# Routing count and experts' bias product given a place in TensorE's order behind the shared expert's first units

## The chip, the cores and the metric

The kernel runs on one core of a Trainium2 chip. The time is device microseconds of one execution. Before the change three runs gave 1411.67, 1405.72 and 1407.75 us, median 1407.75. One further execution was recorded by the profiler; it took 1411.43 us, of which the span from the first to the last instruction is 1409.7 us. Engines are called PE (TensorE), DVE (VectorE), ACT (ScalarE), POOL (GpSimd) and SP (SyncE, which issues most DMAs).

## The reference

Two layers on x of 16 x 256 x 256 (float32): cross-attention, a quantised feed-forward, a correlation attention, and at the end a mixture of experts, where the change lies. Cut to that part:

```python
def _moe_forward(x, Wfc_s, bfc_s, Wproj_s, bproj_s, Wr, Wfc, bfc, Wproj, bproj):
    xf = x.reshape(Bb * Tt, C)                     # 4096 tokens, C = 256, hidden 1024
    shared = new_gelu(xf @ Wfc_s + bfc_s) @ Wproj_s + bproj_s
    logits = xf @ Wr                               # 8 experts
    probs = softmax(logits)
    topk_p, topk_i = top_k(probs, 2)
    topk_p = topk_p / sum(topk_p)
    gate = scatter_add(zeros((N, 8)), topk_i, topk_p)
    routed = 0
    for e in range(8):
        routed += (new_gelu(xf @ Wfc[e] + bfc[e]) @ Wproj[e] + bproj[e]) * gate[:, e:e+1]
    return shared + routed
```

The input of this part is the layer norm of x, and its result is added to x.

## The kernel before

The last part works as follows. A third layer norm of x is transposed into `xnT` (hidden size on the partitions, 4096 tokens along the row), block by block of 512 tokens (`norm3`, transposes at L1351, copies at L1352). `gates(h)` makes the router's logits for half of the tokens each (L1363), turns them back (L1375) and finds the two best experts of every token on DVE (L1384, L1385).

Routing sorts the 8192 pairs of token and expert by expert into tiles of 256 or 128 rows. DVE makes one-hot rows of the choices (`hot`, L1405), adds them, and runs prefix sums over the 32 token tiles (`scan`, L1414 and L1415). What is left is a sum over the 128 partitions, and PE does it: two matmuls `pcount` (L1420 with a triangular matrix, L1421 with ones), copied out as `cnt` (L1423). From `cnt` some 35 small DVE steps compute the start of each expert (`at`), the expert of each tile (`ej`, `ei`), and the slot of each pair (`slot_i`, L1461). `ei` is read by SP into registers, one pair of instructions for each of 46 tiles (L1598), `slot_i` is the index list of the indirect DMAs by which POOL scatters the normalised rows into the DRAM buffer `xs_d` (`scatter`, L1500).

Each tile also needs its expert's hidden bias as a column. `oneT` (L1518) is a one-hot of the tile's expert; eight matmuls `pbias` (L1521) multiply it with the bias table; `bsel` (L1525) is the copy of the product in SBUF. The activations of the routed tiles (L1545, `hTr`) read it.

The shared expert runs in 16 units of 256 tokens. `shared_fc(u)` is the hidden part: 16 matmuls `pfs` (two for each of eight hidden chunks, L1537) and a Gelu on ACT for each chunk (L1545, `hTs`). `shared_proj(u)` is the projection: 16 matmuls `pps` (L1579) and an add onto x on DVE (L1593). A separate DVE add puts the bias row onto x (L1688). Twelve units run ahead of the routed experts, and the hidden part of unit u stands ahead of the projection of unit u-1. The scatters come in eight batches of eight DMAs, and batch k is released by the first activation of unit 3+k (`UB = 3`). Then the routed tiles follow (`routed_fc`, `routed_proj`: weights of the tile's expert by SP, L1600 and L1605, the gathered rows by SP, L1613, transposes L1627, matmuls `pfr` L1537 and `ppr` L1639, a scatter to `ys_d` by POOL, L1665), and at the end the last four shared units beside `combine`, which gathers the two results of every token (L1718) and adds them weighted onto x on DVE (L1726).

The order of the instructions on each engine is chosen by a scheduler, which goes by the program's text as priority and by its estimate of when operands are ready; each engine then works through its list in that order, and an instruction that waits for a semaphore holds the ones behind it. In one earlier stretch PE's order is written out by hand; around this change it isn't. `tc.issue_after(ins)` keeps what is inside it behind `ins` in the list of their engine. In the list of PE before the change the two `pcount` matmuls stand behind two matmuls of unit 0's projection (and a third, which stands earlier, between transposes), with thirteen of them behind; the eight `pbias` matmuls stand in the middle of unit 2's hidden part. PE records show two entries for each float32 matmul.

Of the kernel before, what the change touches and what calls it, by code (L numbers as in the profile page):

```python
# [8 lines left out]
F32 = mybir.dt.float32  # L9
# [3 lines left out]
AF = mybir.ActivationFunctionType  # L13
ALU = mybir.AluOpType
# [4 lines left out]
P = 128  # L19
# [9 lines left out]
def tile_kernel(ctx: ExitStack, tc: tile.TileContext, io: dict, out: bass.AP):  # L29
    nc = tc.nc  # L30
    x_d, ctx_d, mask_d = io["x"], io["ctx_1024"], io["mask_Bx1xSxS2_ik1"]
    B, S, D = x_d.shape
    H, HD = 16, 16
    DC = D // P
    QT = S // P
    NT = B * QT
    F = io["L0_ffn_w1"].shape[0]
    FC = F // P
# [17 lines left out]
    x = big.tile([P, NT, D], F32, tag="x", name="x")  # L56
# [18 lines left out]
    ones = const.tile([P, P], F32, name="ones")  # L75
# [5 lines left out]
    ST = 256  # L81
# [69 lines left out]
    with tc.tile_pool(name="pa", bufs=2) as pa, tc.tile_pool(  # L151
        name="ps_w", bufs=3, space=PSUM
    ) as ps_w, tc.tile_pool(name="ps_o", bufs=1, space=PSUM) as ps_o, tc.tile_pool(
        name="ps_m", bufs=1, space=PSUM
# [559 lines left out]
        bcol = const.tile([P, n_rows], F32, name="bcol")  # L714
        C_B1, C_B2, C_BQ, C_BK, C_BV, C_BFS = cols
# [10 lines left out]
        def load_w(name, eng):  # L726
# [34 lines left out]
        before = const.tile([P, P], F32, name="before")  # L761
        nc.gpsimd.memset(before, 1.0)
        nc.gpsimd.affine_select(
            out=before, in_=before, pattern=[[1, P]], compare_op=ALU.is_gt, fill=0.0, base=0, channel_multiplier=-1
# [18 lines left out]
        bfc8 = const.tile([NE, F], F32, name="bfc8")  # L783
# [23 lines left out]
        pend = None  # L807
        for b in range(B + 1):
# [18 lines left out]
            for r in range(4):  # L827

                n = 4 * b + r
# [11 lines left out]
                pend = (b, r, []) if b < B else None  # L841
# [40 lines left out]
    with tc.tile_pool(name="pb", bufs=2) as pb, tc.tile_pool(  # L882
        name="ps_h", bufs=2, space=PSUM
    ) as ps_h, tc.tile_pool(name="ps_b", bufs=2, space=PSUM) as ps_b, tc.tile_pool(
        name="ps_y", bufs=2, space=PSUM
# [117 lines left out]
        with tc.manual_schedule(engines={mybir.EngineType.PE}):  # L1003
# [3 lines left out]
            for blk in range(NB):  # L1007
                ahead = integers_of(blk + 1) if blk + 1 < NB else iter(())
                for f0 in range(0, FC, 2):
                    ph = ps_h.tile([P, 2, 512], F32, tag="h", name=f"ph1_{blk}_{f0}")  # L1010
# [59 lines left out]
        def second(blk, hq):  # L1070

            yT = pb.tile([P, DC, 512], F32, tag="yT", name=f"yT{blk}")
            for c in range(DC):
                py = ps_y.tile([P, 512], F32, tag="y", name=f"py{blk}_{c}")
                for fc in range(FC):
                    nc.tensor.matmul(
                        py,
                        w2T[:, fc, c * P : (c + 1) * P],
                        hq[:, fc, :],
                        start=(fc == 0),  # L1080
                        stop=(fc == FC - 1),
                    )
                nc.scalar.activation(
                    yT[:, c, :], py, AF.Identity, bias=bq2[:, c : c + 1], scale=s2[:, c : c + 1]
                )
                yield
            for i0 in range(0, TB, 2):
                t = blk * TB + i0
                tp = ps_b.tile([P, 2, D], F32, tag="b", name=f"ytp{blk}_{i0}")
                for i in range(2):  # L1090
                    for c in range(DC):
                        nc.tensor.transpose(
                            tp[:, i, c * P : (c + 1) * P],
                            yT[:, c, (i0 + i) * P : (i0 + i + 1) * P],
                            ident,
                        )
                nc.vector.tensor_tensor(x[:, t : t + 2, :], tp, x[:, t : t + 2, :], ALU.add)
                for i in range(2):
                    ln_stats(mv2, t + i)
                if i0 + 2 == TB:  # L1100
                    ln_rstd(rstd2, mv2, blk * TB, TB, "2")
                yield

        pend = None
        for blk in range(NB + 1):
# [6 lines left out]
            pend = second(blk, hq) if blk < NB else None  # L1112
# [13 lines left out]
    shared_w = load_expert(-1)  # L1126
# [13 lines left out]
    with tc.tile_pool(name="pc", bufs=2) as pc:  # L1140
# [30 lines left out]
        for blk in range(NB):  # L1171
# [3 lines left out]
            q = pc.tile([P, DC, BPB, W], F32, tag="q", name=f"q{blk}")  # L1175
# [10 lines left out]
            for i in range(BPB):  # L1186
                b = blk * BPB + i
                pm = ps_d.tile([P, S], F32, tag="d", name=f"pm{b}")
                n = 0
                for j in range(QT):  # L1190
                    for c in range(DC):
# [4 lines left out]
                            start=(n == 0),  # L1196
                            stop=(n == QT * DC - 1),
# [31 lines left out]
        for c in range(DC):  # L1229
# [4 lines left out]
                start=False,  # L1234
                stop=(c == DC - 1),
# [48 lines left out]
    ps_f = ctx.enter_context(tc.tile_pool(name="ps_f", bufs=4, space=PSUM))  # L1284
    ps_p = ctx.enter_context(tc.tile_pool(name="ps_p", bufs=2, space=PSUM))
    ps_g = ctx.enter_context(tc.tile_pool(name="ps_g", bufs=2, space=PSUM))
    late = ctx.enter_context(tc.tile_pool(name="late", bufs=1))
    pd = ctx.enter_context(tc.tile_pool(name="pd", bufs=2))
# [3 lines left out]
    with tc.tile_pool(name="pe", bufs=2) as pc:  # L1292


        xnT = late.tile([P, DC, NT * P], F32, name="xnT")
# [99 lines left out]
        gates(1)  # L1395

    md_ = ctx.enter_context(tc.tile_pool(name="md_", bufs=1))
    if8 = md_.tile([P, NT, 2], F32, name="if8")  # L1400
# [10 lines left out]
    cur, step = both, 1  # L1411
    while step < NT:
# [3 lines left out]
        cur, step = nxt, 2 * step  # L1416
    rank = md_.tile([P, NT, NE], F32, name="rank")
    nc.vector.tensor_tensor(rank, cur, both, ALU.subtract)
    pq = ps_g.tile([P, 2, NE], F32, tag="g", name="pcount")
    nc.tensor.matmul(pq[:, 0, :], before, cur[:, NT - 1, :], start=True, stop=True)  # L1420
    nc.tensor.matmul(pq[:, 1, :], ones, cur[:, NT - 1, :], start=True, stop=True)  # L1421
    cnt = md_.tile([P, 2, NE], F32, name="cnt")
    nc.vector.tensor_copy(cnt, pq)  # L1423

# [71 lines left out]
    def scatter(t, after):  # L1496
        if t % QT == 0:
            nc.vector.tensor_copy(xn3[t // QT][:, :, 1 + D], if8[:, t : t + QT, 0])
        for k in range(2):
# [13 lines left out]
            )  # L1513
            scatters.append(ins)


    oneT = md_.tile([NE, MT], F32, name="oneT")
    nc.vector.tensor_scalar(oneT, ej[:NE, :], iota_p, None, ALU.is_equal)  # L1518
    pq = ps_g.tile([P, FC, MT], F32, tag="g", name="pbias")
    for fc in range(FC):  # L1520
        nc.tensor.matmul(  # L1521
            pq[:, fc, :], bfc8[:, fc * P : (fc + 1) * P], oneT, start=True, stop=True
        )
    bsel = md_.tile([P, MT, FC], F32, name="bsel")
    nc.vector.tensor_copy(bsel.rearrange("p j f -> p f j"), pq)  # L1525


    first_acts = []

    def hidden_part(wf, rhs, bias, name, n=ST):  # L1530

        hT = pd.tile([P, FC, ST], F32, tag="hT", bufs=3, name="hT" + name)
        acts = []
        for fc in range(FC):
            ph = ps_f.tile([P, ST], F32, tag="f", name=f"pf{name}_{fc}")[:, :n]
            for c in range(DC):
                nc.tensor.matmul(  # L1537
                    ph,
                    wf[:, c, fc * P : (fc + 1) * P],
                    rhs[:, c, :],  # L1540
                    start=(c == 0),
                    stop=(c == DC - 1),
                )
            acts.append(
                nc.scalar.activation(  # L1545
                    hT[:, fc, :n], ph, AF.Gelu_apprx_tanh, bias=bias[:, fc : fc + 1]
                ).ins
            )
        if name[0] == "s":
            first_acts.append(acts[0])  # L1550
        return hT

    NU = NT * P // ST
    U0 = 12
    UB = 3

    def shared_fc(u):
        return hidden_part(
            shared_w[0],
            xnT[:, :, u * ST : (u + 1) * ST],  # L1560
            bcol[:, C_BFS : C_BFS + FC],
            f"s{u}",
        )

    def leave(t):
        b, q = divmod(t, QT)
        nc.sync.dma_start(
            out[b].rearrange("(t p) d -> p t d", p=P)[:, q, :], x[:, t, :]
        )

    def shared_proj(u, hT):
        wp = shared_w[1]
        t0 = 2 * u
        po = ps_p.tile([P, 2, D], F32, tag="p", name=f"pps{u}")
        for i in range(2):
            if u == NU - 1 and i == 1:
                po = ps_p.tile([P, 2, D], F32, tag="p", name=f"pps{u}b")
            for fc in range(FC):
                nc.tensor.matmul(  # L1579
                    po[:, i, :],  # L1580
                    hT[:, fc, i * P : (i + 1) * P],
                    wp[:, fc, :],
                    start=(fc == 0),
                    stop=(fc == FC - 1),
                )
            if u == NU - 1:

                xt = x[:, t0 + i, :]
                nc.vector.tensor_tensor(xt, po[:, i, :], xt, ALU.add)
                leave(t0 + i)  # L1590
        if u < NU - 1:
            xu = x[:, t0 : t0 + 2, :]
            nc.vector.tensor_tensor(xu, po, xu, ALU.add)  # L1593

    def routed_fc(j):
        n = ST if j < NF else HT
# [28 lines left out]
        for c in range(DC):  # L1625
# [4 lines left out]
            xjT[:, :, :n], tp[:, :, :nt, :].rearrange("p c t q -> p c (t q)")  # L1630
        )
        return wp, bj, xj, hidden_part(wf, xjT[:, :, :n], bsel[:, j, :], f"r{j}", n)

    def routed_proj(j, wp, bj, xj, hT):
# [34 lines left out]
                in_offset=None,  # L1669
            )  # L1670

    pend = None
    for u in range(U0):
        hT = shared_fc(u)
        if u == 5:
            with tc.high_priority():
                n_tiles = nc.values_load(nt_i[0:1, 0:1], min_val=1, max_val=MT)
        if UB <= u < UB + NT // 4:
            for t in range(4 * (u - UB), 4 * (u - UB + 1)):
                scatter(t, first_acts[u])  # L1680
        if pend is not None:
            shared_proj(*pend)
        pend = (u, hT)
    shared_proj(*pend)

    for u in range(NU):
        xu = x[:, 2 * u : 2 * u + 2, :]
# [47 lines left out]

    late_ones = list(range(U0))
    share = -(-U0 // (NU - U0))
    pend = None
    for u in range(U0, NU):
        hT = shared_fc(u)  # L1740
# [3 lines left out]
        pend = (u, hT)  # L1744
        n = share + (u > U0)
        if u == NU - 1:
            late_ones.insert(1, u)
            n = len(late_ones)
# [46 lines left out]
```

## Time and profile before

| what | value |
|---|---|
| runs | 1411.67, 1405.72, 1407.75 us |
| profiled execution | 1411.43 us, span 1409.7 us |
| PE busy | 1372.0 us, 97% of the span |
| DVE, ACT, POOL busy | 633.8 (45%), 553.3 (39%), 238.3 (17%) us |
| mean granted clock of PE | 0.994 |
| last prefix sum (L1415) | 702.15 us, 0.28 us long |
| `pcount` (L1420, L1421) | 702.58 to 703.16 us |
| `oneT`, `pbias`, `slot_i` | 710.23, 711.79 to 713.77, 715.37 us |
| first scatter, last scatter | 728.71, 834.21 us |
| first weights of a routed tile | issued at 837.10 us |

Times are microseconds from the start of the span, unless a length is meant. A line of the groups and of the timeline names the engine, the source line, the operation and the tiles (written from read); PEld are the weight loads of PE, which run beside its matmuls. The granted clock is the share of full speed that the clock gate passed to PE in that stretch.

### The profile page before, as it was taken

What the parts mean: (1) busy time and instruction counts of PE and PEld (TensorE: products, weight loads), DVE (VectorE), ACT (ScalarE), POOL (GpSimd) and SP (SyncE); (2) the same over time, 40 slices, a digit from 0 to 9 for tenths busy, and PEclk for the clock granted to TensorE, in tenths of its full rate; (3) what the DMA queues carried; (4) which work ended last, traced back from release to release, by engine and by line L of the source; (5) the groups of instructions that cost most, each with busy time, mean ns of one, the idle gap of its engine ahead of it and who ended that gap; (6) DMA issues with size and microseconds to landing.
All of it is one profiled execution on the core that took longest, in us unless ns stands there. A gap on an engine that the chain in (4) does not pass through costs nothing.

```text
span 1409.7 us, 24104 instructions
## 1 busy us (share of the span) xinstructions
PE 1372.0 (97%) x8955; PEld 1037.8 (74%) x8955; DVE 633.8 (45%) x2519; ACT 553.3 (39%) x1051; POOL 238.3 (17%) x312
## 2 busy tenths in 40 slices
PE   6999999999989999999999999999999999999998
PEld 3566655666647644678688888888888888888887
DVE  7688879887737868857821101011010110101025
ACT  1454544555457568423623232322323223232321
POOL 6142133122000000000025540111111111111110
PEclk9899999999999999999999999999999999999999
DMA  9231333221001100334002235777767677775347
GB/s 269 82 98 54 103 87 86 74 69 31 17 16 39 45 0 1 111 99 96 3 31 72 79 125 205 246 249 227 250 235 260 230 239 245 250 241 178 107 136 238
DMA packets 127831, 184.06 MB, mean 131 GB/s; under 512 B 11600, under 2 KB 104952, under 8 KB 127712
## 3 DMA queue, kind: packets, MB, share of 16 engines
q1 hardware_dynamic: 117600, 152.55, 34.2%
q0 software_dynamic: 10112, 29.94, 6.1%
q8 instruction: 72, 1.18, 0.3%
q14 instruction: 47, 0.39, 0.1%
HBM read 141.16 MB, written 34.48 MB: 125 GB/s over the span
## 4 chain that ended last, share of the span: by engine, by line
PE 84%; DVE 8%; DMA 4%; ACT 2%; issue 1%; SPq 0%; DVEq 0%; ACTq 0%
PE pfr L1537 17%; PE ppr L1639 16%; PE pps L1579 6%; PE pfs L1537 5%; PE sp L500 5%; PE st L568 5%; PE o L601 4%; PE st L578 4%; PE ph L916 3%; PE pm L1192 2%; PE pk L944 2%; DMA ys_d<-yj,to 2%; DMA yg<-ys_d 2%; PE po L1307 2%; PE pp L651 2%; DVE junk L511 2%
## 5 line engine op out<-in xcount | busy, mean ns | idle before, releaser
L1545 ACT ACTIVATE hTr<-pfr,bsel 128x256 f32<-128x256 f32 (+1 forms) x344 | 147.5, 429 | 346.0 <-PE pfr L1537 337.1
L1639 PE MATMUL ppr<-wp,hTr 128*128 128x256 f32 x1088 | 248.5, 379 | 0.0
L1537 PE MATMUL pfr<-xjT,wf 128*128 128x256 f32 (+1 forms) x1376 | 246.6, 338 | 0.7 <-DVE xjT L1629 0.7
L1537 PEld LDWEIGHTS pfr<-xjT,wf 128*128 128x128 f32 x1376 | 215.8, 191 | 30.3 <-issue 9.9
L1647 DVE TENSOR_TENSOR yj<-ppr,bj 128x512 f32<-128x512 f32 (+1 forms) x43 | 24.9, 579 | 440.4 <-PE ppr L1639 440.4
L1639 PEld LDWEIGHTS ppr<-wp,hTr 128*128 128x128 f32 x1088 | 202.2, 190 | 25.0
L511 DVE CUSTOM_DVE_ANT_0 junk<-sp,mb 128x256 bf16<-128x256 f32 x512 | 182.7, 419 | 38.1 <-PE sp L500 37.8
L588 ACT ACTIVATE pT<-st 128x1024 f32<-128x1024 f32 x128 | 124.4, 1021 | 128.4 <-PE st L578 128.4
L1665 POOL DMA_INDIRECT ys_d<-yj,to x68 | 65.2, 959 | 454.4 <-DVE to L1656 241.2
L1545 ACT ACTIVATE hTs<-pfs,bcol 128x256 f32<-128x256 f32 x128 | 59.7, 473 | 145.0 <-PE pfs L1537 141.9
L1537 PE MATMUL pfs<-xnT,wf-1_7251 128*128 128x256 f32 x512 | 114.4, 380 | 0.1
L1579 PE MATMUL pps<-wp-1_7253,hTs 128*128 128x256 f32 x496 | 111.4, 383 | 0.0
L1537 PEld LDWEIGHTS pfs<-xnT,wf-1_7251 128*128 128x128 f32 x512 | 96.6, 190 | 14.2 <-issue 1.4
L1579 PEld LDWEIGHTS pps<-wp-1_7253,hTs 128*128 128x128 f32 x496 | 95.3, 192 | 13.2
L500 PE MATMUL sp<-kT,qT 16*128 16x256 f32 x1024 | 93.1, 421 | 4.0 <-DVE mx L511 3.7
L568 PE MATMUL st<-qT,kT 32*128 32x256 f32 x1024 | 79.6, 409 | 0.7 <-DVE qT L549 0.7
L500 PEld LDWEIGHTS sp<-kT,qT 16*128 16x128 f32 x1024 | 59.2, 193 | 26.7 <-DVE mx L511 9.9
L1500 POOL DMA_INDIRECT xs_d<-xn,slot_i x64 | 61.6, 963 | 93.2 <-ACT hTs L1545 49.9
L601 PE MATMUL o<-pT,cxp 128*32 128x256 f32 x1024 | 73.4, 396 | 1.3 <-ACT pT L588 1.3
L916 PE MATMUL ph<-qT,w1T 128*128 128x512 bf16 x256 | 70.1, 378 | 3.7 <-DVE hmax L1013 1.4
L1593 DVE TENSOR_TENSOR x<-pps,x 128x512 f32<-128x512 f32 x15 | 10.3, 688 | 128.0 <-PE pps L1579 128.0
L578 PE MATMUL st<-mbT,ident 128*128 128x512 bf16 x256 | 67.2, 386 | 0.0
(308 smaller groups left out, 1624.7 us busy)
## 6 DMA issues: line engine op xcount, KB each, us to landing
wf<-in_L_ffn_Wfc_dram SPq DMA_DIRECT2D x43, 1024.0 KB
wp<-in_L_ffn_Wproj_dram SPq DMA_DIRECT2D x43, 1024.0 KB
xs_d<-zero POOLq DMA_DIRECT2D x36, 258.0 KB
yg<-ys_d SPq DMA_DIRECT2D x16, 512.0 KB
xj<-xs_d SPq DMA_DIRECT2D x25, 258.0 KB
bj<-in_L_ffn_bproj_dram SPq DMA_DIRECT2D x43, 128.0 KB
x<-in_x_dram SPq DMA_DIRECT2D x16, 256.0 KB
cx<-in_ctx_dram SPq DMA_DIRECT2D x16, 256.0 KB
```

Of the source, the lines that this page charges most:

```text
L500: nc.tensor.matmul(sps[j // 2][:, j % 2, g, :], pr["qT"][rows, 2 * gp + g, qt * P : (qt + 1) * P], pr["kT"][rows, 2 * gp + g, :], start=Tr ...
L511: order["last"] = done = nc.vector.tensor_tensor_reduce(out=junk, in0=sps[j // 2][:, j % 2, g, :], in1=pr["mb"][:, qt, :], scale=1.0, scal ...
L568: nc.tensor.matmul(tps[j // 2][:, j % 2, k, :], pr["kT"][rows, g, k * P : (k + 1) * P], pr["qT"][rows, g, :], start=(k == 0), stop=False, ...
L578: nc.tensor.matmul(tps[i][:, j].rearrange("p k q -> p (k q)"), ident16, pr["mbT"].rearrange("p k q -> p (k q)"), start=False, stop=True, s ...
L588: nc.scalar.activation(pT, tps[i], AF.Exp)
L601: nc.tensor.matmul(pr["o"][HP * j : HP * (j + 1), g % 2, :], pr["cxp"][:, k, 4 * g + j, :], pTs[j // 2][:, j % 2, k, :], start=(k == 0), s ...
L916: nc.tensor.matmul(ph, w1T[:, c, fc * P : (fc + 1) * P], qT[:, c, blk * 512 : (blk + 1) * 512], start=(c == 0), stop=(c == DC - 1),)
L1537: nc.tensor.matmul(ph, wf[:, c, fc * P : (fc + 1) * P], rhs[:, c, :], start=(c == 0), stop=(c == DC - 1),)
L1545: nc.scalar.activation(hT[:, fc, :n], ph, AF.Gelu_apprx_tanh, bias=bias[:, fc : fc + 1]).ins
L1579: nc.tensor.matmul(po[:, i, :], hT[:, fc, i * P : (i + 1) * P], wp[:, fc, :], start=(fc == 0), stop=(fc == FC - 1),)
L1639: nc.tensor.matmul(po[:, i, :], hT[:, fc, i * P : (i + 1) * P], wp[:, fc, :], start=(fc == 0), stop=(fc == FC - 1),)
L1665: nc.gpsimd.indirect_dma_start(out=ys_d, out_offset=bass.IndirectOffsetOnAxis(ap=to[:, i : i + 1], axis=0), in_=yj[:, i, :], in_offset=None,)
```

## The change

The definitions of the shared expert's helpers (`hidden_part`, `shared_fc`, `leave`, `shared_proj`) move up in the program, ahead of the routing. Units 0 and 1 are written ahead of the routing, unit 2 ahead of the bias product; the loop over the first twelve units starts at 3. `shared_unit(u)` writes the hidden part of u and the projection of u-1 and returns the last matmul of that projection. `pcount` is kept behind the last matmul of unit 0's projection, `pbias` behind that of unit 1's.

```diff
+                last = nc.tensor.matmul(
...
+                ).ins
...
+        return last
+
+    pend = []
+
+    def shared_unit(u):
+
+        pend.append((u, shared_fc(u)))
+        return shared_proj(*pend.pop(0)) if u > 0 else None
+
+    shared_unit(0)
+    turn = shared_unit(1)
...
     pq = ps_g.tile([P, 2, NE], F32, tag="g", name="pcount")
-    nc.tensor.matmul(pq[:, 0, :], before, cur[:, NT - 1, :], start=True, stop=True)
-    nc.tensor.matmul(pq[:, 1, :], ones, cur[:, NT - 1, :], start=True, stop=True)
+    with tc.issue_after(turn):
+        nc.tensor.matmul(pq[:, 0, :], before, cur[:, NT - 1, :], start=True, stop=True)
+        nc.tensor.matmul(pq[:, 1, :], ones, cur[:, NT - 1, :], start=True, stop=True)
...
+    turn = shared_unit(2)
 
     oneT = md_.tile([NE, MT], F32, name="oneT")
     nc.vector.tensor_scalar(oneT, ej[:NE, :], iota_p, None, ALU.is_equal)
     pq = ps_g.tile([P, FC, MT], F32, tag="g", name="pbias")
-    for fc in range(FC):
-        nc.tensor.matmul(
-            pq[:, fc, :], bfc8[:, fc * P : (fc + 1) * P], oneT, start=True, stop=True
-        )
+    with tc.issue_after(turn):
+        for fc in range(FC):
+            nc.tensor.matmul(
+                pq[:, fc, :], bfc8[:, fc * P : (fc + 1) * P], oneT, start=True, stop=True
+            )
...
-    pend = None
-    for u in range(U0):
-        hT = shared_fc(u)
+    for u in range(UB, U0):
+        pend.append((u, shared_fc(u)))
         if u == 5:
...
-        if UB <= u < UB + NT // 4:
+        if u < UB + NT // 4:
...
-        if pend is not None:
-            shared_proj(*pend)
-        pend = (u, hT)
-    shared_proj(*pend)
+        shared_proj(*pend.pop(0))
+    shared_proj(*pend.pop(0))
```

In the built order of PE the sixteen `pps` matmuls of unit 0 stand together, `pcount` behind them, then unit 2's hidden part, unit 1's projection, `pbias`, and unit 3's hidden part. On ACT one of the copies into `xnT` (the first half of block 6) is gone; it is on DVE. On DVE the add of unit 0's projection stands ahead of `cnt` and an add of the bias row behind it, `slot_i` ahead of `bsel`, and the small copies of the choices into the rows to be scattered (L1498) all ahead of `cnt`. The lists of POOL and SP have the same order as before.

More of the change, by code (lines that the diff above doesn't have):

```diff
@@ L1395, in tile_kernel, with hidden_part @@
         gates(1)
+    first_acts = []
+    def hidden_part(wf, rhs, bias, name, n=ST):
+        hT = pd.tile([P, FC, ST], F32, tag="hT", bufs=3, name="hT" + name)
+        acts = []
+        for fc in range(FC):
+            ph = ps_f.tile([P, ST], F32, tag="f", name=f"pf{name}_{fc}")[:, :n]
+            for c in range(DC):
+                nc.tensor.matmul(
+                    ph,
+                    wf[:, c, fc * P : (fc + 1) * P],
+                    rhs[:, c, :],
+                    start=(c == 0),
+                    stop=(c == DC - 1),
+                )
+            acts.append(
+                nc.scalar.activation(
+                    hT[:, fc, :n], ph, AF.Gelu_apprx_tanh, bias=bias[:, fc : fc + 1]
+                ).ins
+            )
+        if name[0] == "s":
+            first_acts.append(acts[0])
+        return hT
@@ new lines, in tile_kernel, with shared_fc, leave, shared_proj @@
+    NU = NT * P // ST
+    U0 = 12
+    UB = 3
+    def shared_fc(u):
+        return hidden_part(
+            shared_w[0],
+            xnT[:, :, u * ST : (u + 1) * ST],
+            bcol[:, C_BFS : C_BFS + FC],
+            f"s{u}",
+        )
+    def leave(t):
+        b, q = divmod(t, QT)
+        nc.sync.dma_start(
+            out[b].rearrange("(t p) d -> p t d", p=P)[:, q, :], x[:, t, :]
+        )
+    def shared_proj(u, hT):
+        wp = shared_w[1]
+        t0 = 2 * u
+        po = ps_p.tile([P, 2, D], F32, tag="p", name=f"pps{u}")
+        for i in range(2):
+            if u == NU - 1 and i == 1:
+                po = ps_p.tile([P, 2, D], F32, tag="p", name=f"pps{u}b")
+            for fc in range(FC):
+                last = nc.tensor.matmul(
+                    po[:, i, :],
+                    hT[:, fc, i * P : (i + 1) * P],
+                    wp[:, fc, :],
+                    start=(fc == 0),
+                    stop=(fc == FC - 1),
+                ).ins
+            if u == NU - 1:
+                xt = x[:, t0 + i, :]
+                nc.vector.tensor_tensor(xt, po[:, i, :], xt, ALU.add)
+                leave(t0 + i)
+        if u < NU - 1:
+            xu = x[:, t0 : t0 + 2, :]
+            nc.vector.tensor_tensor(xu, po, xu, ALU.add)
+        return last
@@ L1519, in tile_kernel @@
     pq = ps_g.tile([P, FC, MT], F32, tag="g", name="pbias")
-    for fc in range(FC):
-        nc.tensor.matmul(
-            pq[:, fc, :], bfc8[:, fc * P : (fc + 1) * P], oneT, start=True, stop=True
-        )
+    with tc.issue_after(turn):
+        for fc in range(FC):
+            nc.tensor.matmul(
+                pq[:, fc, :], bfc8[:, fc * P : (fc + 1) * P], oneT, start=True, stop=True
+            )
     bsel = md_.tile([P, MT, FC], F32, name="bsel")
     nc.vector.tensor_copy(bsel.rearrange("p j f -> p f j"), pq)
-    first_acts = []
@@ L1530, in hidden_part @@
[L1530 to L1593, printed above, removed]
```

## The prediction

> **What bounds the kernel now.** I read first the waits of TensorE (PE) from the router's end to the end of the span: who released it, us in total, times, longest us.
>
> ```profile
> engine line waited for: us in total, times, longest us
> PE pcount L1420 <- DVE xn L1498: 1.8, 1, 1.8
> PE pfr L1537 <- DVE xjT L1629: 0.7, 1, 0.7
> PE x3tp L1351 <- ACT xn L1341: 0.6, 1, 0.6
> PE pps15b L1579 <- DVE x L1593: 0.2, 1, 0.2
> ```
>
> In 730 us PE waits four times, 3.3 us in all. So from about 680 us on the span is the sum of PE's instructions, and what PE loses or gains there reaches the end. The longest wait is that of the count, the first product that the change moves. The chain of waits around it, in order of time (start, us, what):
>
> ```profile
> 702.24 0.20 DVE scan L1415
> 702.43 0.16 DVE xn L1498 x2
> 702.60 0.34 PE pcount L1420 x2
> 702.94 0.22 PE pcount L1421 x2
> 703.16 7.40 PE pps L1579 x26
> 710.57 1.29 PE pfs L1537 x6
> 711.86 1.91 PE pbias L1521 x16
> 713.77 5.81 PE pfs L1537 x26
> 719.58 6.91 PE pps L1579 x32
> ```
>
> Up to the count the chain is VectorE's (DVE) routing, behind it PE's stream without a break. Two records make one matmul of the list here. The reader should compare rates: a full projection is 32 records in 6.91 us, 0.216 us each; the 26 records right behind the count take 7.40 us, where 26 x 0.216 = 5.62. Something made them 1.78 us slower. Busy time by stretch shows it (stretch, its length, PE busy and instructions, granted PE clock, DMA share, GB/s):
>
> ```profile
> 698.00:700.00 2.00, 2.00 (x11) 1.00 0.00 0
> 700.00:702.00 2.00, 0.76 (x4) 1.00 0.00 0
> 702.00:704.00 2.00, 1.42 (x7) 0.84 0.03 8
> 704.00:706.00 2.00, 2.00 (x6) 0.50 0.00 0
> 706.00:708.00 2.00, 2.00 (x9) 0.81 0.00 0
> 708.00:710.00 2.00, 2.00 (x11) 1.00 0.01 4
> ```
>
> Behind the gap the clock is halved for some 3.4 us: the loss is 2 x (0.16 + 0.50 + 0.19) = 1.70 us, about the 1.78 found in the records. So the wait costs twice: 1.82 us of standing still and 1.7 to 1.8 us of half speed.
>
> **The change part by part.** *The count.* In the built order of PE all 16 matmuls of unit 0's projection now stand ahead of the count, where before three of them did (two right ahead of it, one earlier among the transposes). The work is the same; only the order differs. PE comes to the end of the projection at 710.57 - 1.82 (gap) - 1.78 (half clock) - 0.56 (count) = 706.4 us. The last prefix sum ends at 702.43. So the count finds its operand 4.0 us old, and the gap goes: -1.82. Without a gap there is no half clock behind it: -1.78.
>
> The count also waits on PE's own semaphore, as it did before. Now the matmul ahead of it is a projection that has only just been issued, so its end may have to be awaited: a record lasts 379 ns where one is issued every 216, so 0.16 us; I take +0.16, bounds 0 and 0.38 (one whole record). The third unit's projection has a PE wait where it had a DVE wait; what it waits for is 14 us old, 0.
>
> *What the count's delay makes late.* The count moves from 702.60 to 706.4. On DVE, the copy of it is now behind the add of unit 0's projection (0.60) and has an add of the bias row (0.60) behind it; six small copies (0.07 each) have gone ahead of it. The copy starts at about 707.2 (before 703.20). From there to the one-hot's start took 7.03 us (703.20 to 710.23); now 7.03 + 0.60 - 0.4 = 7.2, so it is ready at 714.6. The slots come some 1.1 us behind, near 715.8: before, 715.37, because there they stood behind the bias copy that waited 2.10 us for PE.
>
> Who waits? The first scatter, on GpSimd (POOL), is released by unit 3's first activation, not by the slots:
>
> ```profile
> 728.71 1.20 POOL L1500 DMA_INDIRECT xs_d<-xn,slot_i  x1 [48.42 <-ACT hTs L1545]
> ```
>
> It comes 3.4 us earlier, about 725.3; the slots have 9 us of slack. SyncE's 43 loads of expert numbers (710.3 to 735.0) start and end 4 us later, near 739; the first expert's weights are not issued before 837.10, held by the last scatter's landing, so 95 us of cover hide them. Cost 0.
>
> *The bias product.* Its 16 records (1.91 us) move from inside unit 2's hidden part to behind unit 1's projection. PE gets there at 706.4 + 0.16 + 0.56 + 6.91 + 6.91 = 720.9; its operand has been there since 714.6, a cover of 6.3 us. Its result, used first near 860, is hidden by 130 us. Cost 0. Were the cover gone, PE's queue would stop in front of it, and all of unit 3 behind.
>
> *The stretch 684 to 693 us.* One copy of a transposed block (0.6 us) goes from ScalarE to DVE, where a later add waited 0.56 us anyway; one projection matmul changes places with one of the next hidden part, whose buffer is free at about 689 and which PE reaches at 690. I take 0, bounds -0.6 and +0.6 (the 0.6 us wait in the first table that might go, or come a second time).
>
> *Sum.* -1.82 - 1.78 + 0.16 + 0 + 0 = -3.44 us. The profiled execution took 1411.43 us (span 1409.7): 1408.0. Its tail lies 3.7 us above the median of the runs, 1407.75; the gap lies in a stretch ruled by PE, so I take the same amount off the median: 1404.3. Bounds of the terms: with half clock in none of the runs and the worst of the rest -1.82 + 0.38 + 0.6 = -0.84; with the best -1.82 - 1.78 - 0.6 = -4.2.
>
> *A rule against it.* The half clock is not behind each gap here: 1.10 us idle before 197.73 us is followed by 0.54 and 0.60, 1.14 before 41.70 by 0.50, but 2.51 before 31.53 by 1.00. The Trainium skill ("TensorE: Matmul & The Clock Gate", "HAM oscillation — how this bites in real kernels") says that the clock falls behind idle gaps above some 3.4 us, and its Part 1 that the watching window runs freely. By that rule a gap of 1.82 us costs no clock, and the sum would be -1.66. The rows 198 to 202 and 704 to 706 disagree, at gaps a third to half as long; that a longer gap went free agrees with a free-running window.
>
> **The rivals.**
> *The half clock is not this gap's* (the rule above, or a phase that the runs without a profile mostly miss). Then only the gap is gained: -1.82 + 0.16 = -1.66, 1406.1. For it: 2.51 us went free. Against: of the four gaps above 1 us named here three were followed by it, and this one at once.
> *The tail takes it back.* The last unit's projection waits 0.25 us for DVE, which waits for gathers. If the gathers' chain set the end by itself, PE would wait 0.25 + 3.44 there, gain 0, 1407.75. Against: that chain starts when the last routed tile has been scattered (issue 1353.77), and that is PE's stream too, so both shift together.
> *Slower: PE stops in front of the bias product.* It stands in order in PE's queue, at 720.9. If the one-hot came g us later than that, PE would idle g and pay the half clock again: -3.44 + g + 1.78. It turns into a loss at g = 1.7, that is with the one-hot at 722.6, 8 us later than worked out; at g = 4.0 it is 1407.75 + 2.3 = 1410.1. For it: the routing chain is some 40 dependent DVE steps. Against: their durations are in the trace, and only two adds of 0.60 come between.
> *It does not do what it says*: the count would still have PE stand. The built order excludes that for the gap of 702 us, as far as scan and stream keep their times: 4.0 us.
>
> **How the numbers follow.** Forecast (-3.44) 0.70, gap alone 0.12, tail takes it 0.08, slower by the bias product 0.06, more than -4.2 (a second dip that goes too) 0.04. The predicted time is 1404.3. The runs before lie between 1405.72 and 1411.67, 6 us apart, so a median of three may be off by some 2 to 3 us; this is wider than any term. Forecast less 4 gives 1400.3, and the slower case with its noise reaches 1410: the range is 1400.3 to 1409.8. Faster or slower means by over 0.5% (7 us), about what a measurement of this kernel can tell from no change. All cases' centres lie within 0.5%, so only noise and what I missed lie outside: same 0.82, faster 0.10 (forecast and more, below 1400.7), slower 0.08 (the bias case with g above 9, or a cost not seen).
>
> **What would show it.** PE's waits after 680 us: the count's 1.8 is gone, nothing above 0.7 is new. The stretches from 700 to 710 have clock 1.00 and PE busy throughout; unit 0's projection takes 6.91 us in one piece. The count starts near 706.4, the bias product near 720.9, the first scatter near 725.3, the first routed tile's transpose 3.4 us before 857.5. Wrong would be: a new wait before bias product or count, a clock below 1.00 behind 690 us, or a wait of the last projection that has grown from 0.2 to 3 us.

## The result and the profile after

Twenty runs of the changed kernel have a median of 1404.71 us, twenty of the kernel before 1408.81 us. The ratio is 0.9973, with a 95% interval from 0.9964 to 0.9983: 2.4 to 5.1 us less. The profiled execution took 1407.56 us, span 1405.9.

TensorE's waits after 680 us in the changed kernel (who released it, total, times, longest):

```profile
engine line waited for: us in total, times, longest us
PE pps15b L1449 <- DVE x L1463: 1.3, 1, 1.3
PE pfr L1407 <- DVE xjT L1643: 0.7, 1, 0.7
PE x3tp L1351 <- ACT xn L1341: 0.6, 1, 0.6
PE pps L1449 <- DVE x L1463: 0.3, 1, 0.3
```

The 1.8 us wait of the count is gone. Nothing has come in its place near it, but the last unit's projection, at the end of the kernel, now waits 1.3 us where it waited 0.2. TensorE's timeline around the count (start, length):

```profile
697.55 7.07 PE L1449 MATMUL pps<-wp-1_7253,hTs 128*128 128x256 f32 x32
704.45 0.28 PE L1500 MATMUL pcount<-scan,before 128*128 128x8 f32 x2
704.59 0.37 PE L1501 MATMUL pcount<-scan,ones 128*128 128x8 f32 x2
704.82 7.15 PE L1407 MATMUL pfs<-xnT,wf-1_7251 128*128 128x256 f32 x32
711.81 7.07 PE L1449 MATMUL pps<-wp-1_7253,hTs 128*128 128x256 f32 x32
718.81 1.98 PE L1603 MATMUL pbias<-oneT,bfc 8*128 8x46 f32 x16
```

Starts follow each other at the full rate: 704.45 - 697.55 = 6.90 us for the 32 records of unit 0's projection, with no gap ahead of the count. The stretches agree (length, PE busy, granted clock, DMA share, GB/s):

```profile
700.00:702.00 2.00, 2.00 (x11) 1.00 0.00 0
702.00:704.00 2.00, 2.00 (x11) 1.00 0.00 0
704.00:706.00 2.00, 2.00 (x13) 1.00 0.00 0
706.00:708.00 2.00, 2.00 (x11) 1.00 0.00 0
```

PE is busy throughout and the clock is 1.00, where it was 0.84, 0.50 and 0.81 from 702 to 708 us. What the count's delay made late:

```profile
705.26 0.17 DVE L1503 COPY cnt<-pcount 128x16 f32<-128x16 f32 x1
712.79 0.23 DVE L1599 TENSOR_SCALAR oneT<-ej,iota_p 8x46 f32<-8x46 f32 x1
714.29 0.20 DVE L1541 CAST slot_i<-slot 128x64 uint32<-128x64 f32 x1
```

The one-hot is ready (713.02) 5.8 us before the bias product starts (718.81), and the slots (714.49) 8.7 us before the first scatter (723.21).

To compare executions I use one stretch of PE's stream, from the start of the router's second product (`pl`) to the start of the first routed tile's transpose (`xjtp`). It holds everything that the change moves behind the router. Its first and last lines, before and then after:

```profile
690.43 1.92 PE L1363 MATMUL pl<-xnT,wr 128*32 128x512 f32 x16
857.55 0.82 PE L1627 MATMUL xjtp<-ident,xj 128*128 128x128 f32 x6
```

```profile
688.67 1.92 PE L1363 MATMUL pl<-xnT,wr 128*32 128x512 f32 x16
852.05 0.82 PE L1641 MATMUL xjtp<-ident,xj 128*128 128x128 f32 x6
```

Before, the stretch took 167.12 us; after, 163.38 us: **3.74 us less**. The profiles' other differences lie outside: 1.76 us were already there at `pl`, for the most part a wait of the first scores near 24 us, in work that the change does not touch (2.18 us before, 0.70 after), and 1.70 us were lost behind `xjtp`, in the tail (552.15 us to the end of the span before, 553.85 after). 1.76 + 3.74 - 1.70 = 3.8, the difference of the spans. Both outer parts differ as much between executions of kernels that are nearly alike there: over the ten profiles of this document `pl` starts between 684.57 and 690.43 us.

### The profile page after: what moved, and what is told of

The parts are those of the page before. It is cut to its first block, busy times and chain, and to the rows that moved or that the text cites. A ratio compares the mean times of both kernels' runs of the same rounds, so it can differ in the third digit from the quotient of the medians.

```text
span 1405.9 us, 24030 instructions
## 1 busy us (share of the span) xinstructions
PE 1358.8 (97%) x8881; PEld 1035.8 (74%) x8955; DVE 633.8 (45%) x2520; ACT 553.3 (39%) x1050; POOL 239.0 (17%) x312
## 5 line engine op out<-in xcount | busy, mean ns | idle before, releaser
L1449 PEld LDWEIGHTS pps<-wp-1_7253,hTs 128*128 128x128 f32 x496 | 94.2, 190 | 13.5 <-DVE x L1463 0.7
L568 PEld LDWEIGHTS st<-qT,kT 32*128 32x128 f32 x1024 | 50.7, 186 | 18.2 <-issue 12.4
```

The source lines that it names most:

```text
L568: nc.tensor.matmul(tps[j // 2][:, j % 2, k, :], pr["kT"][rows, g, k * P : (k + 1) * P], pr["qT"][rows, g, :], start=(k == 0), stop=False, ...
L1449: last = nc.tensor.matmul(po[:, i, :], hT[:, fc, i * P : (i + 1) * P], wp[:, fc, :], start=(fc == 0), stop=(fc == FC - 1),).ins
```

## The experiments

### The count put back, the bias product left in its new place

Which of the two moved products brings the gain? Here the count stands behind three projection matmuls again, and the rest of unit 0's projection behind it.

```diff
     shared_unit(0)
-    turn = shared_unit(1)
+    pend.append((1, shared_fc(1)))
+    u0, h0 = pend.pop(0)
...
+    with tc.issue_after(last_hidden[-1]):
+        turn = part0(mm0[:2])
...
     with tc.issue_after(turn):
-        nc.tensor.matmul(pq[:, 0, :], before, cur[:, NT - 1, :], start=True, stop=True)
+        nc.tensor.matmul(pq[:, 0:NE], before, cur[:, NT - 1, :], start=True, stop=True)
...
+    with tc.issue_after(turn):
+        turn = part0(mm0[2:])
```

(`part0` is unit 0's projection in parts, `mm0` its list of matmuls. The third matmul ahead of the count is one of unit 1's projection. The tile of the count is wider than it needs; a later experiment uses the room.)

> The changed kernel with the count put back behind three projection matmuls; the bias product stays behind unit 1's projection. Measured by the stretch of TensorE's stream from the start of the router's second product to the first transpose of a routed tile: 167.1 us before the change (690.43 to 857.55), 163.4 after it (688.67 to 852.05). Theory (the wait of the count and the half clock behind it are the whole gain): a wait of 1.8 us at the count, clock 0.50 for 3.4 us behind it, stretch 167.1, time as before the change (ratio 1.000). Rival (the new place of the bias product brings the gain): stretch 163.4, ratio 0.997.

The wait came back (1.8 us), the stretch was 687.16 to 854.27, 167.11 us, and twelve runs had a median of 1408.68 us, ratio 0.999 (0.9978 to 1.0003) to the kernel before. In the stretch the bias product's new place alone brings nothing, and the count's brings everything. The times agree with that, but their interval overlaps that of the changed kernel (0.9964 to 0.9983), so they do not show it by themselves. The clock behind the gap, in stretches:

```profile
698.00:700.00 2.00, 0.69 (x5) 1.00 0.00 0
700.00:702.00 2.00, 2.00 (x6) 0.53 0.04 8
702.00:704.00 2.00, 2.00 (x7) 0.62 0.00 0
```

It fell to half again, for a loss of 2 x (0.47 + 0.38) = 1.70 us.

### The same kernel profiled again

> The kernel with the count put back, a second profile of it. Theory (a gap of 1.8 us always brings the half clock): clock 0.50 behind it, stretch 167.1 us. Rival (it depends on where the gap falls in a clock window that runs freely): now and then clock 1.00, stretch 165.3 to 165.4 us.

One execution. The same gap of 1.82 us, and behind it:

```profile
698.00:700.00 2.00, 0.73 (x4) 1.00 0.00 0
700.00:702.00 2.00, 1.44 (x9) 1.00 0.00 0
702.00:704.00 2.00, 2.00 (x11) 1.00 0.03 8
```

The clock stayed at 1.00, and the stretch was 688.40 to 853.84, 165.44 us: 1.67 less than with the half clock. So the two costs are separate: standing still was paid in each of the three profiles that have this gap (before, and these two), the half clock in two of them.

### The gap filled with matmuls of no use

Against the kernel with the count put back:

```diff
+    with tc.issue_after(turn):
+        for _ in range(4):
+            turn = nc.tensor.matmul(
+                pq[:, 32:288], h0[:, 0, :P], shared_w[1][:, 0, :], start=True, stop=True
+            ).ins
     with tc.issue_after(turn):
         nc.tensor.matmul(pq[:, 0:NE], before, cur[:, NT - 1, :], start=True, stop=True)
```

> As the kernel with the count put back, but four matmuls of no use (same shape as the projection's, 0.432 us each by the records before) stand in TensorE's queue ahead of the count, in the 1.8 us in which it stood still. Theory (standing still halves the clock): no wait above 0.3 us, clock 1.00 from 690 to 720 us, stretch 163.4 + 1.73 + 0.2 = 165.3 us, so 1.8 us less than before the change. Rival (the half clock comes from something else at that place, such as the small matmuls of the count): clock 0.50 behind the count as before, stretch 167.1 us.

A wait of 0.52 us was left (one projection matmul fewer stood ahead than before the change), more than expected. The clock stayed at 1.00 throughout:

```profile
696.00:698.00 2.00, 1.60 (x8) 1.00 0.00 0
698.00:700.00 2.00, 1.88 (x11) 1.00 0.03 8
```

The stretch was 685.97 to 851.83, 165.86 us: 2.48 more than the changed kernel (1.73 of matmuls, 0.52 of waiting, 0.23 of the rest) and 1.26 less than before the change, although the count starts as late as before, 12.15 us behind `pl` in both. The small matmuls of the count do not halve the clock by themselves: they ran here, and in the changed kernel, at 1.00. Since the clock now and then holds behind the gap too, one profile does not prove that the filling kept it up; it agrees with it. The time, 1407.69 us, ratio 0.9998 (0.9983 to 1.0012), is too blunt to show 1.26 us.

### A shorter gap, twice

Five matmuls ahead of the count in place of three (`mm0[:5]`).

> As the kernel with the count put back, but five projection matmuls ahead of it instead of three, so that the wait is 1.82 - 2 x 0.432 = 0.96 us. Theory (a gap of about 1 us is enough): clock 0.50 for some 3.4 us behind it, stretch 163.4 + 0.96 + 1.78 = 166.1 us. Rival (only longer gaps count): clock 1.00, stretch 164.3 us.

> The kernel with the gap of 0.95 us, a second profile of it. Theory (a gap of about 1 us never brings the half clock at this place): clock 1.00, stretch 164.6 us. Rival (it depends on where the gap falls, as with the gap of 1.10 us near 195 us, which brought it in three profiles of six): clock 0.50 behind it in some profiles, stretch 166.3 us.

The waits were 0.95 and 0.96 us, the clock 1.00 both times, the stretches 164.57 and 164.56 us. The expectation of a half clock behind 1 us failed. But a gap of that size cannot be called safe: the gap of 1.10 us near 195 us, which all these programs share, was followed by a clock near 0.5 in five of the ten profiles and by 1.00 in the other five. The time of the first was 1405.41 us, ratio 0.9972 (0.9959 to 0.9986), not to be told from the changed kernel's.

### The bias product back in its old place

```diff
+    def bias_product(behind):
+        with tc.issue_after(behind):
+            for fc in range(FC):
+                edge = nc.tensor.matmul(
+                    pq[:, fc, :], bfc8[:, fc * P : (fc + 1) * P], oneT, start=True, stop=True
+                ).ins
...
-    turn = shared_unit(2)
+    pend.append((2, shared_fc(2, bias_product)))
+    with tc.issue_after(last_bias[-1]):
+        shared_proj(*pend.pop(0))
```

(`bias_product` is called behind the second hidden chunk of unit 2; the rest of the unit is kept behind it.)

> The changed kernel with the bias product back inside unit 2's hidden part, four matmuls behind the count, as it stood before. Theory (the delayed count makes the routing chain late, so the bias product has to move with it): TensorE reaches it at 706.6 us by the times of the changed kernel, its operand comes at 713.0; wait 6.4 us, half clock behind it, stretch 163.4 + 6.4 + 1.8 = 171.6 us, some 8 us above the changed kernel and 4 above the one before. Rival (the place of the bias product does not matter): stretch 163.4 us.

Its wait, and stretches around it:

```profile
PE pbias L1609 <- DVE oneT L1603: 6.3, 1, 6.3
```

```profile
706.00:708.00 2.00, 0.00 (x0) 0.68 0.01 4
708.00:710.00 2.00, 1.04 (x5) 0.50 0.00 0
...
714.00:716.00 2.00, 2.00 (x6) 0.50 0.00 0
716.00:718.00 2.00, 2.00 (x8) 0.76 0.00 0
```

The clock fell while PE still stood, and stayed at half until some 717 us. The stretch was 684.57 to 858.12, 173.55 us, 10.2 above the changed kernel: 6.3 of waiting and 3.9 of half clock, where 1.8 were expected. Four runs had a median of 1418.16 us, ratio 1.0068 (1.0048 to 1.0087). This is the slower rival of the prediction, made real: with the count late, the bias product has to be late too. That is what the second move saves, and why it shows no gain of its own. The medians lie 13.5 us apart, 3 more than this profile's stretch explains; the profiled execution was the fastest of the four (1411.43 us), and with so few runs the rest stays open.

### Half a unit's projection left out

```diff
+            nf = FC // 2 if u == 5 else FC
-            for fc in range(FC):
+            for fc in range(nf):
...
-                    stop=(fc == FC - 1),
+                    stop=(fc == nf - 1),
```

The kernel leaves out the last four of the eight hidden chunks of unit 5.

> The changed kernel with half of unit 5's projection left out: 8 of its 16 matmuls, 8 x 0.432 = 3.45 us of TensorE (the last four hidden chunks are not summed, so x of 256 tokens lacks them). It tells whether an amount of TensorE time of the size of the change reaches the end. Theory (TensorE's stream sets the end from 680 us on): stretch 163.4 - 3.45 = 159.9 us, time 3.4 us below the changed kernel, ratio to before 0.995. Rival (the tail takes it back): stretch 159.9 us too, but the wait of pps15b grows by 3.4 us and the time stays, ratio 0.997.

The stretch was 686.92 to 846.84, 159.92 us, as expected. Four runs: 1402.97 us, ratio 0.9949 (0.9933 to 0.9964) where the changed kernel has 0.9973 (0.9964 to 0.9983): the intervals just touch, and the difference of 0.0024, 3.4 us, is the amount left out. So it reached the end, though this profile has a wait of 2.0 us at `pps15b`. That wait is not the price of an earlier stream: over the ten profiles it goes from none to 2.0 us without regard to when the first routed transpose starts (none at 851.86 and at 858.12, 2.0 at 846.84 and at 852.85).

### The last projection in a bank of its own

`ps_p` and `ps_g` are the kernel's pools of tiles for TensorE's products. In `ps_p` the last half unit has to wait until DVE has added the product that stands in its tile (the wait of `pps15b` for `x`).

```diff
-                po = ps_p.tile([P, 2, D], F32, tag="p", name=f"pps{u}b")
+                po = ps_g.tile([P, 2, D], F32, tag="g", name=f"pps{u}b")
```

> The changed kernel with the last half unit's projection (pps15b) written to a PSUM bank of the routers' pool, so that TensorE no longer waits there for VectorE to clear the bank of unit 14. Theory (the tail took back part of the gain in the changed kernel's profile, by the 1.3 us wait of pps15b and 0.3 us of pps): no wait at pps15b; the last matmul ends 0.3 to 1.3 us earlier, measured from the first transpose of a routed tile to the end of the span 551.6 to 552.6 us where the changed kernel had 553.9; time 1404.0 us or a little less. Rival (the gathers set the end by themselves): the span ends where it did, 553.9 us behind that transpose, ratio to before 0.997.

The wait of `pps15b` is gone and PE ends at 1400.2 us, but the span ends 554.0 us behind the first routed transpose, where the changed kernel had 553.9. The chain that ended last:

```profile
1388.53 7.62 DMA yg<-ys_d
1396.15 0.03 issue
1396.17 2.87 DVE x L1737 x7
```

The last gather took 7.62 us in this execution (5.87 in the profile of before, 5.76 in that of after), and DVE's adds behind it set the end. So in this execution the gathers set the end, as the rival has it. But its last gather was 1.86 us longer than that in the profile of after, so it does not tell what the wait of `pps15b` cost there; that stays open. The time, 1406.05 us, ratio 0.9966 (0.9955 to 0.9977), overlaps with that of the changed kernel; no gain over it is shown.

## Why the prediction was right

**The bound.** That PE's stream sets the end from 680 us on is shown by the projection left out (3.46 us less in the stretch, ratio 0.9949 against 0.9973) and by the bias product put early. The last few us belong to the gathers: the chain that ended last goes over a gather and DVE's adds behind it in eight of the ten profiles, before and after among them. The prediction's argument that both shift together is shown too: the first gather was issued 500.0 to 500.5 us behind the first routed transpose in all ten, although that transpose started anywhere from 846.84 to 858.12.

**The gap, -1.82.** Right: gone after the change, back to 1.8 us with the count put back.

**The half clock, -1.78.** Right in its mechanism for the profiled executions, too certain for the runs: with the same gap it was absent in one profile of three. Its count of earlier gaps (three of four followed by half clock) left out two of the same trace: 2.18 us before 23.90 and 1.45 us before 140.81, both followed by 1.00. It is three of six, and the 0.12 for the gap alone was low on that evidence. How often the half clock is paid can be estimated from the mean granted clock of all runs. 29 runs of the kernel before, beside the first experiments, have 0.99545 on average, the twenty of the changed kernel 0.9965: times the span (0.00455 x 1408) = 6.4 us against (0.0035 x 1404) = 4.9 us of lost clock, 1.5 us less. Seventeen more runs of the kernel before, beside the later experiments, have 0.9950, and the twelve of the last projection in its own bank, taken beside them, 0.9965: 2.1 us. Single runs lie between 0.992 and 0.999, and the twelve with the gap filled have 0.9972 on average, above the changed kernel, so each difference is unsure by about 1 us. Both agree with 1.7 us paid in most runs, but do not prove it.

**The count's wait for PE itself, +0.16.** Not paid: the count starts 6.90 us behind the projection's start, the bare sum of its records. So the stretch lost 3.74 us, against -1.82 - 1.78 = -3.60 without that term.

**What comes late: cost 0.** Right. The one-hot and the slots were ready 1.6 and 1.3 us earlier than worked out (713.02 for 714.6, 714.49 for 715.8), as this execution was 1.76 us ahead at the router. The covers of 6.3 and 9 us were 5.8 and 8.7. The bias product put early shows what stands on that cover, and that the rival's price (the gap and 1.78) was too low: behind 6.3 us of standing still the half clock cost 3.9.

**684 to 693 us: 0.** No new wait there; the one of 0.6 stayed.

**The tail.** The prediction expected no new wait above 0.7 us; `pps15b` shows one of 1.3, short of the 3 that it named as a sign of being wrong. The rival's place was right, its mechanism not: the tail varies from execution to execution (551.6 to 555.8 us from the first routed transpose to the end, ten profiles), and took 1.70 us in the profile of after, but an earlier stream is not what makes it longer: the same start of the stream (852.05, 851.86) was followed by 553.85 and by 551.64 us.

**The sum.** -3.44 was forecast; the medians of twenty differ by 4.1, with 2.4 to 5.1 in the interval. That the time itself came so close (1404.3 forecast, 1404.71 measured) is partly luck: the median before, from three runs, was 1.06 us below that of twenty, and the change was 0.66 us larger than forecast. The profiled execution (1408.0 forecast, 1407.56 measured) came close because the 1.76 us gained elsewhere and the 1.70 us lost in the tail cancel.

## What to carry to other kernels

An engine's list is a queue: a small instruction that waits stops all work behind it, and moving it behind work that is ready costs nothing as long as those who need its result have cover. When one is moved, work out when its result is ready now, and move whatever in the same queue waits for that result along with it: here the second product cost 10 us of the stretch when it stayed in its old place. A gap in TensorE's stream is to be priced with the clock behind it, by the rate of the matmuls that follow, and since that part comes and goes between executions, by more than one profile.

## What was unexpected

A gap of 1.10 us near 195 us was followed by half clock in five profiles of ten, one of 1.82 us in two of three, two of about 0.95 us not at all; 6.3 us of standing still cost 3.9 us of half clock, over twice the 1.7 of the shorter gaps. Nor does the length alone decide: a gap of 1.45 us near 140 us, in six of the profiles, and one of 2.5 us near 30 us, in all ten, were followed by 1.00 each time. The Trainium skill ("TensorE: Matmul & The Clock Gate", "HAM oscillation — how this bites in real kernels") puts the limit at some 3.4 us; these runs disagree, with halved clock behind gaps a third as long. Part 1 of that page of the Trainium skill says that the window runs freely and the result varies by run; the five of ten agree with it. The tail can pay it too: in the second profile of the short gap `pps15b` waited 2.01 us and its 16 records then took 5.41 us, where behind waits of 1.26, 1.32, 1.78 and 2.02 us in four other profiles they took 3.72.
